# A graph network layer on one core: five buffers of rows of x, loaded ahead, and single rows fetched by SyncE for two more blocks

## The chip, the core and the metric

The kernel runs on one core of one Trainium2 chip. The time is device microseconds for one execution. A core has five engines, each with its own in-order queue of instructions: TensorE (PE in the profile; PEld are its weight loads) multiplies matrices, VectorE (DVE) and ScalarE (ACT) work elementwise, GpSimd (POOL) here only issues gathers, and SyncE (SP) here only issues transfers between memory and the on-chip buffers. An engine that waits for a semaphore holds up everything behind it in its own queue.

## The reference, cut to what matters

There are N = 8192 nodes with C = 256 features, and E = 131072 edges, sorted by their target, with 64 features each.

```
ea  = edge_attr @ w_e + b_e
msg = relu(x[src] + ea)                       # 131072 x 256: a gather of rows of x
agg = segment_sum(msg, dst, num_segments=N)
h_local = bn(relu((x + agg) @ w1 + b1) @ w2 + b2 + x)
h_attn  = bn(attention in groups of 32 nodes, 4 heads, of x, with in_w and out_w) + x, scaled likewise
out = h_local + h_attn
out = bn(out + relu(out @ m_w1 + m_b1) @ m_w2 + m_b2)
result = layernorm(x + out)
```

All of it is fp32. The batch norms (bn) are a scale and a shift for each feature.

## The kernel before, in words

**Edges.** The edges are worked on in 128 blocks of 1024 (BE). For a block, GpSimd issues eight indirect transfers, each of which gathers 128 rows of x into the tile xs (`gather`, line 217; the tile has six buffers). SyncE loads the block's edge features in four transfers (`load_edges`, line 261, tile ea, four buffers, up to four blocks ahead). VectorE transposes them in squares of 32 (line 299, tile eaT), TensorE multiplies them by w_e into PSUM (`edge_products`, tile pe), VectorE adds the gathered rows (`edge_messages`, line 357), ScalarE takes the relu (line 361). VectorE builds a one-hot matrix from the relative targets `rel` (`edge_hot`, line 369, tile oh), TensorE sums the messages with it (`group_sums`, tile pw), ScalarE copies the sums out (`edge_sums`, line 405, tile ws, two buffers), and TensorE places them by a second one-hot product (`edge_place`, tile l), which VectorE adds to the transposed x of the right nodes (line 431, tile xT).

**Single rows.** In the blocks of the list FETCHED (six in number, from 44 to 98) the eighth gather is left out. Its 128 rows are fetched by SyncE, one transfer of 1 KB for each row, from addresses that SyncE reads into registers: `row_stream`, line 239, tile xf with two buffers, in steps of four rows. A step is issued whenever the scheduler calls `between`, as long as there is a quota, and from about block 26 on each block adds three steps (RUN) to the quota. In these blocks the last addition is made in three pieces (line 351), two from xs and one from xf.

**Nodes.** The nodes are worked on in 16 chunks of 512 (CH). For a chunk, the rows of x are loaded by SyncE into the tile xn (`load_nodes`, line 438, four buffers). `attention_front` turns them by TensorE (line 178) into xT and computes q and k; `attention_back` computes v, the attention and its output product; `dense`, once all edges of the chunk are placed, computes the two layers of the local part and the two of the final one, adds the rows of xn at the end (line 748, the last reader of xn), normalises, and stores the result (line 765). The last two chunks are cut into smaller parts (`dense` of half chunks and `dense_rows`).

**Order.** TensorE's order is written out by the program while it is built. The class Work holds four streams of generators (dense parts, fronts, backs, and the second dense stream of the end); each `yield` gives the estimated time of what was just issued. Until block 24 (NV) VectorE's and ScalarE's order is written out too (`stated`). Up to block 104 (TAIL) blocks go in pairs, and `run` hands out a share of work between the steps of the edges. The last 24 blocks go singly: a planner with an assumed time at which each block's rows have come (`came`) decides what is next, and `step` hands out the node work between.

Some yields are signals. LOAD, from line 580, says that a front has just issued the load of its own rows: in the middle part the front's stream then rests until the program's own clock has gone on by 10 us (FAR), in the first part for two rounds, in the last part for 6 us. AFTER makes the back's stream wait for the next block, by the counter `told`, which counts only in the first part.

From chunk 4 on a front may begin only when `dense` of the chunk four before has been issued to its end. It then finds no rows of x loaded, issues the load (which on the chip waits until line 748 of that dense part has run, because the buffer is the same), and yields LOAD.

**Holding the gathers.** After the order is built, `hold_fetches` ties each gather to a matmul: the n-th gather waits for the last matmul whose estimated time lies 10 us (AHEAD) or more before n times 1.254 us.

Of the kernel before, what the change touches and what calls it, by code (L numbers as in the profile page):

```python
# [41 lines left out]
RUN = 3  # L42
FETCHED = [44, 54, 64, 76, 86, 98]
FROM = 26
# [44 lines left out]
def gnn_kernel(ctx: ExitStack, tc: tile.TileContext, x, src, dst, edge_attr, w, out):  # L89
# [27 lines left out]
    srci = const.tile([P, NB, TB], I32, name="srci")  # L117
    rel = const.tile([P, NB, TB], FP, name="rel")
    wrow = const.tile([P, NB], FP, name="wrow")
# [69 lines left out]
    def hold_fetches():  # L189
# [3 lines left out]
        for n, fetch in fetches:  # L193
# [8 lines left out]
            if i:  # L202
# [3 lines left out]
                )  # L206

    def gather(b):
        xs = epool.tile([P, NH, TJ, C], FP, name="xs", tag="xs", bufs=BUFS)
        for h in range(NH):  # L210
            for j in range(TJ):
                if b in FETCHED and h * TJ + j == TB - 1:
                    continue
                idx = srcd[:, b * NH + h, j : j + 1] if b < ND else srci[:, b, h * TJ + j : h * TJ + j + 1]
                fetches.append((
                    b * TB + h * TJ + j,
                    nc.gpsimd.indirect_dma_start(  # L217
                        out=xs[:, h, j, :],
                        out_offset=None,
                        in_=x if b < NX else xb[:, :],  # L220
                        in_offset=bass.IndirectOffsetOnAxis(ap=idx, axis=0),
                    ).ins,
                ))
        xs_of[b] = xs

    last_src = const.tile([P, P], I32, name="last_src")
    xf_of = {}

    def row_stream():

        for b in FETCHED:
            xf = xf_of[b] = epool.tile([P, C], FP, name="xf", tag="xf", bufs=2)
            for r in range(QR):
# [4 lines left out]
                for m, row in enumerate(rows):  # L238
                    nc.sync.dma_start(xf[m * QR + r : m * QR + r + 1, :], xb[ds(row, 1), :])  # L239
                yield  # L240

# [50 lines left out]
    def between():  # L292
        for do in spots:
            do()
# [39 lines left out]
    def edge_messages(b, pairs=range(0, NH, 2), of_pair=range(2)):  # L334
# [6 lines left out]
        for h in pairs:  # L341
            pe = pe_of[b, h]
            for u in of_pair[::n]:
                hs = slice(h + u, h + u + n)
                if h + u + n == NH and b in FETCHED:
                    for us, js, rows in (
                        (slice(0, 2), slice(0, TJ - 1), xs[:, h:]), (slice(0, 1), slice(TJ - 1, TJ), xs[:, h:]),
# [48 lines left out]
    def edge_sums(blocks):  # L396
# [3 lines left out]
        if pw is None:  # L400
            pw = pps.tile([P, 2, C], FP, name="pw", tag="at", bufs=4)
            for i, b in enumerate(blocks):
                group_sums(pw, i, b, [(h, j) for j in range(TJ) for h in range(NH)])
        ws = epool.tile([P, 2, C], FP, name="ws", tag="ws", bufs=2)
        newest["ws"] = nc.scalar.copy(ws[:, :n], pw[:, :n]).ins  # L405
# [27 lines left out]
    chunk = [{} for _ in range(NCH)]  # L433
    stated = [True]

    def load_nodes(n0, st, pool):
        xn = st["xn"] = pool.tile([P, TN, C], FP, name="xn", tag="xn", bufs=4)
        nc.sync.dma_start(xn, x[ds(n0, CH), :].rearrange("(t p) c -> p t c", p=P))
# [251 lines left out]
    def dense(n0, st, pool, bank, a=0, z=CH, own=("h1", "m1", "zT", "y", "")):  # L690

        assert st["done"]
        w, cs = z - a, slice(a, z)
        tiles = [(t // P, min(P, w - t)) for t in range(0, w, P)]
# [175 lines left out]
    class Work:  # L870
# [15 lines left out]
        def may(self, i):  # L886
            s = self.streams[i]
            return s and not self.rest[i] and self.told >= self.after[i] and clock[0] >= self.free[i] and s[0][0]()

# [29 lines left out]
        def step(self, t, until):  # L919

            n = len(self.streams)
            for i in [k % n for k in range(self.turn, self.turn + n)]:
                while self.streams[i] and self.streams[i][0][0]() and t >= self.at[i]:
# [4 lines left out]
                    elif d in (REST, LOAD):  # L928
                        self.at[i] = t + 6.0
                    elif d > 0:  # L930
                        t += d
                        self.at[i], self.turn = t + 0.5, (i + 1) % n
                        return t
            later = [a for a, q in zip(self.at, self.streams) if q and q[0][0]() and a > t]
# [13 lines left out]
    with tc.manual_schedule(engines={PE}):  # L948
# [136 lines left out]

        came = [8.7 + 10.035 * (i + 1) for i in range(NB)]
        t, l, s = came[b - 2] + 20, b - 2, b - 2
# [82 lines left out]
    hold_fetches()  # L1170
    fast.close()


# [121 lines left out]
```

## Time and profile before

| | |
|---|---|
| Median of 3 runs | 1645.59 us (1641.8 to 1648.5) |
| The profiled execution | 1641.08 us, span of its instructions 1639.3 us |
| Mean granted TensorE clock | 0.914 of full speed |
| DVE, ACT busy in the span | 805.6 us (49%), 591.8 us (36%) |
| Transfers | 240.62 MB, mean 147 GB/s |
| Gathers issued by GpSimd (line 217) | 858 + 144 + 16 = 1018 |
| Row transfers issued by SyncE (line 239) | 768 |
| Loads of chunks of x (line 438) | 16, the last at 1378.4 us |

The span runs from the first to the last instruction. A group of instructions is shown with its line, engine, operation, the names of its output and inputs, its count, its busy time, the mean of one in ns, and the idle time just before it with what ended that. A wait is shown as the engine and line that waited, what it waited for, the total, how often, and the longest. Times of instructions count from the span's start. The granted clock is TensorE's, as a share of full speed.

### The profile page before, as it was taken

What the parts mean: (1) busy time and instruction counts of PE and PEld (TensorE: products, weight loads), DVE (VectorE), ACT (ScalarE), POOL (GpSimd) and SP (SyncE); (2) the same over time, 40 slices, a digit from 0 to 9 for tenths busy, and PEclk for the clock granted to TensorE, in tenths of its full rate; (3) what the DMA queues carried; (4) which work ended last, traced back from release to release, by engine and by line L of the source; (5) the groups of instructions that cost most, each with busy time, mean ns of one, the idle gap of its engine ahead of it and who ended that gap; (6) DMA issues with size and microseconds to landing.
All of it is one profiled execution on the core that took longest, in us unless ns stands there. A gap on an engine that the chain in (4) does not pass through costs nothing. (4 is left out here: it accounts for less than half of the span.)

```text
span 1639.3 us, 24510 instructions
## 1 busy us (share of the span) xinstructions
PE 1330.6 (81%) x7591; PEld 762.6 (47%) x7591; DVE 805.6 (49%) x1649; ACT 591.8 (36%) x842; POOL 966.1 (59%) x1026
## 2 busy tenths in 40 slices
PE   3778769788987888778887588879799898878777
PEld 2444444444543545345553354445445454444555
DVE  5266664436454364345553355354455546364543
ACT  1334333333434344243442334324344343433333
POOL 5665656466666566656666465656666656656662
PEclk9888889899999999889998799889899899999899
DMA  9679755445545464454544545445565655454531
GB/s 240 181 220 262 222 148 148 131 130 152 152 126 164 112 163 129 127 150 132 150 127 126 136 130 147 123 130 145 132 164 138 160 124 163 128 142 123 148 97 50
DMA packets 150339, 240.62 MB, mean 147 GB/s; under 512 B 28638, under 2 KB 113788, under 8 KB 149436
## 3 DMA queue, kind: packets, MB, share of 16 engines
q0 software_dynamic: 48864, 133.50, 29.9%
q1 hardware_dynamic: 100252, 105.51, 23.3%
q8 instruction: 62, 1.02, 0.3%
q14 instruction: 73, 0.60, 0.1%
q10 hardware_dynamic: 1088, 0.00, 0.0%
HBM read 222.13 MB, written 16.78 MB: 146 GB/s over the span
## 5 line engine op out<-in xcount | busy, mean ns | idle before, releaser
L217 POOL DMA_INDIRECT xs<-xb,srci x858 | 811.9, 946 | 535.6 <-issue 211.3
L361 ACT ACTIVATE xs<-xs 128x1024 f32<-128x1024 f32 (+2 forms) x253 | 263.6, 1046 | 424.2 <-DVE xs L357 275.6
L357 DVE TENSOR_TENSOR xs<-pe,xs 128x1024 f32<-128x1024 f32 (+2 forms) x253 | 298.0, 1203 | 171.7 <-PE at L174 51.0
L174 PE MATMUL pe<-we,eaT 64*128 64x256 f32 x2048 | 314.0, 431 | 80.4 <-issue 39.3
L174 PEld LDWEIGHTS pe<-we,eaT 64*128 64x128 f32 x2048 | 211.7, 208 | 189.3 <-issue 105.6
L174 PE MATMUL pw<-xs,oh 128*32 128x256 f32 x2048 | 192.4, 416 | 53.0 <-issue 48.9
L217 POOL DMA_INDIRECT xs<-in_x_dram,srci x144 | 137.1, 952 | 95.5 <-issue 37.2
L369 DVE TENSOR_TENSOR oh<-iota_n,rel 128x128 f32<-128x128 f32 x256 | 65.4, 293 | 238.6 <-PE pw L174 94.6
L174 PEld LDWEIGHTS pw<-xs,oh 128*32 128x32 f32 x2048 | 71.3, 115 | 166.4 <-issue 132.7
L174 PE MATMUL at<-xT,inT 128*128 128x512 f32 x256 | 123.6, 609 | 5.4 <-issue 4.1
L174 PE MATMUL at<-hA,mw 128*128 128x512 f32 (+1 forms) x256 | 120.7, 599 | 3.3 <-DVE hA L714 1.4
L174 PE MATMUL at<-m,mw 128*128 128x512 f32 (+1 forms) x256 | 115.7, 594 | 8.8 <-ACT m L721 3.9
L174 PE MATMUL l<-oh,ws 128*128 128x160 f32 (+4 forms) x512 | 86.3, 309 | 30.3 <-ACT ws L405 15.0
L174 PEld LDWEIGHTS l<-oh,ws 128*128 128x128 f32 x512 | 75.3, 198 | 64.4 <-issue 35.0
L299 DVE STREAM_TRANSPOSE eaT<-ea 128x512 f32<-128x512 f32 x128 | 89.4, 699 | 30.3 <-PE at L174 9.8
L405 ACT COPY ws<-pw 128x512 f32<-128x512 f32 (+1 forms) x77 | 39.4, 511 | 151.7 <-remote 53.6
L640 ACT COPY pr<-pe 32x256 f32<-32x256 f32 x128 | 46.5, 363 | 91.8 <-remote 45.6
L174 PEld LDWEIGHTS at<-m,mw 128*128 128x128 f32 x256 | 48.4, 197 | 63.2 <-issue 53.9
L174 PE MATMUL at<-oT,outT 128*128 128x512 f32 x128 | 72.0, 691 | 6.5 <-ACT oT L675 3.8
L174 PEld LDWEIGHTS at<-xT,inT 128*128 128x128 f32 x256 | 47.6, 194 | 63.0 <-issue 55.7
L174 PE MATMUL at<-xT,w 128*128 128x512 f32 (+1 forms) x128 | 66.5, 655 | 11.4 <-DVE xT L431 8.6
L431 DVE TENSOR_TENSOR xT<-l,xT 128x352 f32<-128x352 f32 (+14 forms) x107 | 43.3, 427 | 59.4 <-remote 30.7
(163 smaller groups left out, 1270.2 us busy)
## 6 DMA issues: line engine op xcount, KB each, us to landing
ea<-in_edge_attr_dram SPq DMA_DIRECT2D x512, 128.0 KB
xs<-xb,srci POOLq DMA_INDIRECT x858
xf<-xb SPq DMA_DIRECT2D x768, 1.0 KB
xn<-in_x_dram SPq DMA_DIRECT2D x16, 512.0 KB
out_dram<-y SPq DMA_DIRECT2D x14, 512.0 KB
xp<-in_x_dram SPq DMA_DIRECT2D x10, 512.0 KB
xb<-xp SPq DMA_DIRECT2D x10, 512.0 KB
xp<-in_x_dram SPq DMA_DIRECT2D x3, 1024.0 KB
```

The source lines that it names most:

```text
L174: mark(ps, nc.tensor.matmul(ps, *args, **kw).ins)
L217: nc.gpsimd.indirect_dma_start(out=xs[:, h, j, :], out_offset=None, in_=x if b < NX else xb[:, :], in_offset=bass.IndirectOffsetOnAxis(ap= ...
L299: nc.vector.transpose(eaT, ea[:, QR:].rearrange("p (g d) -> p g d", d=ED)[:, :, :QR])
L357: nc.vector.tensor_add(msg[:, hs, js].rearrange("p u i c -> p i u c"), pe[:, js, u : u + n, :], xs[:, hs, js].rearrange("p u i c -> p i u c"),
L361: nc.scalar.activation(msg[:, hs, js], msg[:, hs, js], AF.Relu)
L369: nc.vector.tensor_tensor(oh[:, ts], iota_n[:, None, :WN].to_broadcast([P, TB // 2, WN]), rel[:, b, ts, None].to_broadcast([P, TB // 2, WN ...
L405: newest["ws"] = nc.scalar.copy(ws[:, :n], pw[:, :n]).ins
L431: newest["xT"] = nc.vector.tensor_add(xT, l2[:, :, a - n : z - n], xT).ins
L640: nc.scalar.copy(pr[q, :, 2 * hh : 2 * hh + 2, :].rearrange("p t s k -> p s t k"), two4[q, :, :, q])
```

## The change

- `xn` has five buffers instead of four. To make room, `ws` has one instead of two, and `rel` is bf16 instead of fp32 (its values are small whole numbers).
- `dense` of chunk c, when it begins, issues the load of the rows of chunk c + 4 (for chunks 4 to 15). The front of that chunk then finds its rows loaded and yields no LOAD. The first four chunks load as before.
- FETCHED also names blocks 108 and 117. So 1016 gathers and 1024 row transfers are issued. As these two blocks lie in the last 24, the planner's `step` now calls `between` too, so that rows are issued there, and a check is added that a block's rows have all been issued.
- `skipped(b)` counts the blocks of FETCHED from TAIL up to b. The planner's assumed arrival times (`came`) and the numbers by which later gathers are held are moved earlier by 1.254 us for each.
- A stream that waits for the next block (AFTER) is let go when the first part ends.

```
-FETCHED = [44, 54, 64, 76, 86, 98]
+FETCHED = [44, 54, 64, 76, 86, 98, 108, 117]
...
-    rel = const.tile([P, NB, TB], FP, name="rel")
+    rel = const.tile([P, NB, TB], BF, name="rel")
...
+    def skipped(b):
+        return sum(TAIL <= i <= b for i in FETCHED)
...
-                    b * TB + h * TJ + j,
+                    b * TB + h * TJ + j - skipped(b - 1),
...
+                if r == QR - 1:
+                    all_of.add(b)
...
+                    assert b in all_of
...
-        ws = epool.tile([P, 2, C], FP, name="ws", tag="ws", bufs=2)
+        ws = epool.tile([P, 2, C], FP, name="ws", tag="ws")
...
-        xn = st["xn"] = pool.tile([P, TN, C], FP, name="xn", tag="xn", bufs=4)
+        xn = st["xn"] = pool.tile([P, TN, C], FP, name="xn", tag="xn", bufs=5)
...
     def dense(n0, st, pool, bank, a=0, z=CH, own=("h1", "m1", "zT", "y", "")):
         assert st["done"]
+        if fast_path[0] and not a and n0 // CH + 4 < NCH:
+            load_nodes(n0 + 4 * CH, chunk[n0 // CH + 4], pool)
...
-            return s and not self.rest[i] and self.told >= self.after[i] and clock[0] >= self.free[i] and s[0][0]()
+            return s and not self.rest[i] and (self.told >= self.after[i] or not stated[0]) and clock[0] >= self.free[i] and s[0][0]()
...
                         self.at[i], self.turn = t + 0.5, (i + 1) % n
+                        between()
                         return t
...
-        came = [8.7 + 10.035 * (i + 1) for i in range(NB)]
+        came = [8.7 + 10.035 * (i + 1) - 1.254 * skipped(i) for i in range(NB)]
```

More of the change, by code (lines that the diff above doesn't have):

```diff
@@ L226, in gnn_kernel @@
     last_src = const.tile([P, P], I32, name="last_src")
-    xf_of = {}
+    xf_of, all_of = {}, set()
     def row_stream():
@@ L433, in gnn_kernel @@
     chunk = [{} for _ in range(NCH)]
-    stated = [True]
+    stated, fast_path = [True], [True]
     def load_nodes(n0, st, pool):
-        xn = st["xn"] = pool.tile([P, TN, C], FP, name="xn", tag="xn", bufs=4)
+        xn = st["xn"] = pool.tile([P, TN, C], FP, name="xn", tag="xn", bufs=5)
         nc.sync.dma_start(xn, x[ds(n0, CH), :].rearrange("(t p) c -> p t c", p=P))
@@ L1171, in gnn_kernel @@
     fast.close()
+    fast_path[0] = False
     wide = nc.values_load(width[0:1, 0:1])
```

## The prediction

> **What bounds the kernel now.** I read the page first, then who waited for whom on TensorE, then the instructions in order of time around the two longest waits, then the busy time by stretches. The page's head and the group of gathers:
>
> ```profile
> span 1639.3 us, 24510 instructions
> PE 1330.6 (81%) x7591; PEld 762.6 (47%) x7591; DVE 805.6 (49%) x1649; ACT 591.8 (36%) x842; POOL 966.1 (59%) x1026
> L217 POOL DMA_INDIRECT xs<-xb,srci x858 | 811.9, 946 | 535.6 <-issue 211.3
> ```
>
> TensorE is busy for 1330.6 of 1639.3 us and idle for 308.7. GpSimd is busy for only 59%, though the schedule in the code is written as if its gathers were the clock (10.035 us for each block of eight). How fast do the gathers really come? Two stretches of the gathers alone, the first from block 28 to the end of block 91, the second from block 96 to the end of block 123 (columns: length, POOL busy and count, clock, DMA share, GB/s):
>
> ```profile
> 373.50:1173.60 800.10, 479.70 (x507) 0.91 0.51 138
> 1220.90:1566.60 345.70, 211.02 (x223) 0.94 0.51 138
> ```
>
> The 507 gathers are 64 blocks of eight less five that SyncE replaced, 12.50 us a block; the 223 are 28 blocks less one, 12.35 us a block. So neither stretch runs at the gathers' pace. Each gather is held in the code until TensorE has reached a certain matmul, so the gathers follow TensorE, and I count what TensorE loses. Anything that leaves TensorE idle in its in-order queue in the middle of the kernel should reach the end almost in full.
>
> Most of its 308.7 idle us are small change: a few tenths between one operand's arrival and the next. Two single waits stand out, both by the transposes of a newly loaded chunk of x (tile xn, line 178); the waits of two windows:
>
> ```profile
> PE at L178 <- DMA xn<-in_x_dram: 5.3, 1, 5.3
> PE at L178 <- DMA xn<-in_x_dram: 16.2, 1, 16.2
> ```
>
> In order of time, first round the shorter wait and then round the longer one (start, duration, engine, line):
>
> ```profile
> 701.55 1.29 DVE L748 TENSOR_TENSOR y<-at,xn 128x512 f32<-128x512 f32 x2 [2.24 <-remote]
> 714.02 1.76 SPq L261 DMA_DIRECT2D ea<-in_edge_attr_dram  x4
> 718.97 0.28 SPq L438 DMA_DIRECT2D xn<-in_x_dram  x1
> 721.77 1.29 DVE L299 STREAM_TRANSPOSE eaT<-ea 128x512 f32<-128x512 f32 x2
> 724.03 1.97 PE L178 MATMUL at<-ident,xn 128*128 128x128 f32 x8 [5.26 <-DMA xn<-in_x_dram]
> ...
> 900.34 1.29 DVE L748 TENSOR_TENSOR y<-at,xn 128x512 f32<-128x512 f32 x2 [2.41 <-PE at L174]
> 907.87 2.14 SPq L261 DMA_DIRECT2D ea<-in_edge_attr_dram  x4
> 914.89 1.29 DVE L299 STREAM_TRANSPOSE eaT<-ea 128x512 f32<-128x512 f32 x2
> 915.61 1.80 SPq L261 DMA_DIRECT2D ea<-in_edge_attr_dram  x4
> 919.79 0.41 SPq L438 DMA_DIRECT2D xn<-in_x_dram  x1
> 924.38 1.97 PE L178 MATMUL at<-ident,xn 128*128 128x128 f32 x8 [16.20 <-DMA xn<-in_x_dram]
> ```
>
> The buffer of xn comes free when line 748 has added x to the last result of an old chunk: at 702.84 and at 901.63. The load is issued 16.1 and 18.2 us later, because SyncE issues in order and stands behind the loads of edge rows (line 261), which themselves wait for VectorE to transpose an older tile:
>
> ```profile
> SPq L261 <- DVE oh L369: 11.2, 1, 11.2
> ```
>
> Then the load needs 4.6 to 5.1 us to land, and TensorE, whose queue has the transposes next, stands. In the other ten of the twelve loads from chunk 4 on, the pause that the code puts behind a load (10 us of its own reckoning) covered it.
>
> **The change part by part.** *The early load.* With five buffers the load of chunk c+4 is issued at the beginning of the dense layers of chunk c. Its buffer is then that of chunk c-1, whose last reader is done or nearly so, and the transposes come behind the whole dense part of chunk c, tens of us later. The load is moved past the SyncE loads and the output store that stood ahead of it; nothing that was ahead of it needs it. So both waits go: 5.3 + 16.2 = **-21.5 us**.
>
> What comes after them goes too. Busy time and clock in the four us after each wait and the four after that (columns: length, then PE, PEld, DVE, ACT, POOL busy, granted clock, DMA share, GB/s), and the same eight transposes where nothing was late:
>
> ```profile
> 724.00:728.00 4.00, 3.97 (x11) 2.78 (x12) 0.00 (x0) 2.68 (x4) 0.00 (x0) 0.50 0.41 147
> 728.00:732.00 4.00, 4.00 (x10) 1.71 (x9) 0.00 (x0) 1.37 (x2) 1.90 (x2) 0.97 0.18 53
> 924.00:928.00 4.00, 3.62 (x24) 2.17 (x24) 0.00 (x0) 2.41 (x4) 0.00 (x0) 0.50 0.19 63
> 928.00:932.00 4.00, 4.00 (x37) 2.61 (x34) 2.51 (x4) 0.97 (x2) 2.35 (x3) 0.79 0.17 41
> 1208.14 1.04 PE L178 MATMUL at<-ident,xn 128*128 128x128 f32 x8
> ```
>
> After each wait TensorE worked at a granted clock of 0.50, and its eight transposes took 1.97 us for 1.04. What it lost is 4 x (0.50 + 0.03 + 0.50 + 0.21) = **-5.0 us**. The Trainium skill, page "TensorE: Matmul & The Clock Gate", section "Part 1: The HAM clock gate", says that an idle window of about 3.4 us halves the clock and that it takes about 3.4 us of work to get it back. By that figure the two waits would have cost 2 x 1.7 = 3.4 us instead of 5.0, and the sum below would be 1.6 us smaller; the 0.50 in the rows agrees with the rule.
>
> Against that stands what the kernel made good after a wait, since the gathers and VectorE had run ahead. The stretch from the transposes to the next line 748, after a load that wasn't late and after the two late ones:
>
> ```profile
> 522.80:585.00 62.20, 54.18 (x309) 30.42 (x306) 29.70 (x54) 24.76 (x36) 36.87 (x39) 0.92 0.48 128
> 724.00:782.00 58.00, 52.08 (x292) 31.18 (x294) 25.36 (x45) 22.53 (x32) 32.41 (x35) 0.90 0.48 132
> 924.40:986.00 61.60, 56.27 (x335) 33.12 (x336) 28.38 (x54) 25.98 (x37) 35.51 (x38) 0.90 0.48 128
> ```
>
> TensorE idles 12.9%, 10.2% and 8.7%. The difference, 2.7% of 58.0 and 4.2% of 61.6, is 4.2 us that were already won back: **+4.2 us**.
>
> *No pause behind the load.* The attention stream of the next chunk no longer stops for 10 us of reckoning behind its load, so its matmuls can fill that stretch. The first and the last of ten such stretches, from line 748 to the transposes, without the two above:
>
> ```profile
> 296.00:307.00 11.00, 4.43 (x9) 1.64 (x8) 6.15 (x20) 3.09 (x4) 5.06 (x6) 0.75 0.81 213
> 1377.00:1388.00 11.00, 8.28 (x46) 4.28 (x47) 9.21 (x25) 4.60 (x7) 6.49 (x7) 1.00 0.54 172
> ```
>
> All ten are 141.9 us long with 29.1 us idle; at 12.9% it would be 18.3. So 10.8 us is the most that filling them can give. The work that moves in is missing later in the same chunk, and the next dense part can't open before its edges are added up, so that some of the idleness only moves; a loss is bounded by the same size. I take **-3 us** of 0 to -10.8, nearer to none since about half of the excess (6.57 - 1.42 = 5.1 us) lies in the first stretch alone.
>
> *Two gathers fewer.* Blocks 108 and 117 lose one gather each, 946 ns of GpSimd: at most -1.9 us where GpSimd is the late one in the last stretch, nothing where TensorE is. I take **-1 us**. That the later gathers are let go 1.25 and 2.5 us earlier in the reckoning, and that the planner of the last 24 blocks expects them as much earlier, is the same gain seen from the other side and isn't counted again.
>
> In return the last addition of those two blocks is made in three pieces. The whole one, and the pieces as they ran in the six blocks that have them now (the second number behind the bar is the mean in ns):
>
> ```profile
> L357 DVE TENSOR_TENSOR xs<-pe,xs 128x1024 f32<-128x1024 f32 x248 | 295.3, 1216 | 171.3 <-PE at L174 51.0 <-issue 27.2 <-PE pw L174 26.2
> L351 DVE TENSOR_TENSOR xs<-pe,xs 128x512 f32<-128x512 f32 x6 | 4.1, 681 | 1.0 <-PE pw L174 1.0
> L351 DVE TENSOR_TENSOR xs<-pe,xf 128x256 f32<-128x256 f32 x6 | 2.5, 413 | 0.0
> L351 DVE TENSOR_TENSOR xs<-pe,xs 128x256 f32<-128x256 f32 x6 | 2.5, 413 | 0.0
> L369 DVE TENSOR_TENSOR oh<-iota_n,rel 128x128 f32<-128x128 f32 x256 | 65.4, 293 | 238.6 <-PE pw L174 94.6 <-remote 68.4 <-PE pe L174 45.6
> ```
>
> 681 + 413 + 413 - 1216 = 291 ns, twice: **+0.6 us**, if VectorE is waited for both times.
>
> *256 more single rows.* They are SyncE transfers of one row each, 64 steps of four, three steps to a block, so they occupy SyncE in some 21 more blocks: today's stream ends at 1195.6 us and would now end some 21 x 12.35 = 260 us later, near 1460. What such rows take in SyncE's queue, at their usual and at their slowest, and the edge loads that stand behind them:
>
> ```profile
> L239 SPq DMA_DIRECT2D xf<-xb x768: 2/228/1387, 253.1 to 1195.6; - x192
> ...
> xf<-xb SPq DMA_DIRECT2D x768, 1.0 KB
> 637.82 7.90 SPq L239 DMA_DIRECT2D xf<-xb  x12
> 878.60 14.41 SPq L239 DMA_DIRECT2D xf<-xb  x12
> 893.11 1.76 SPq L261 DMA_DIRECT2D ea<-in_edge_attr_dram  x4
> ```
>
> Behind a late row stand the next edge rows and the output stores; who waits for those is VectorE's transposition (line 299) and then TensorE. The cover is that edge rows are loaded up to four blocks ahead. I take 0: the stretch with rows at 12.50 us a block contains the 21.5 us of the two waits, and without them it is (800.1 - 21.5) / 64 = 12.17, not slower than the 12.35 of the stretch that has almost no rows. If the cover fails, see the last rival.
>
> *The rest at nothing.* The one-hot comparison (line 369) reads a bf16 operand instead of fp32 and still writes fp32; it took 293 ns, and a tenth either way would be 256 x 29 ns = 7.5 us on VectorE, which is 49% busy, so a us or two at the end. With one buffer instead of two for ws, ScalarE's copy must wait for the matmuls that read the former ws; these stand ahead of the sums that the copy reads anyway in TensorE's in-order queue, so the wait is over before it begins. The relaxed rule for a stream that waits for the next block, once the written-out order ends, adds no instruction.
>
> The sum: -21.5 - 5.0 + 4.2 - 3.0 - 1.0 + 0.6 = **-25.7 us**. The profiled execution took 1641.08 us with its span of 1639.3, so it would take 1615.4. The median of the runs shown is 1645.59, 4.5 above it, so I forecast **1620 us** for the runs.
>
> **The rivals.** *More is filled.* If all ten stretches fill up (-10.8), nothing had been made good (0 for +4.2) and both gathers count, the sum is -21.5 - 5.0 - 10.8 - 1.9 + 0.6 = -38.6: 1607 us. For it speaks that the order gets smoother in every chunk; against it, that a dense part still waits for its edges.
>
> *Another wait stands behind the one removed.* VectorE's transposes of edge rows (line 299) ended at 721.77 + 1.29 = 723.1 us and at 914.89 + 1.29 = 916.2, that is 4.3 and 8.0 us into the two waits (which began at 724.03 - 5.26 = 718.8 and at 908.2). If the edge products come next in TensorE's order and these transposes are as late as before, only 21.5 - 12.3 = 9.2 us go. Half the clock loss stays (-2.5), half the catch-up (+2.1), and the sum with the small terms at none is -9.6 + 0.6 = -9.0: 1637 us, at the edge of no difference. For it: VectorE sat idle in the longer wait itself. Against it: the chunk's own sixteen attention matmuls come first and give TensorE some 10 us of work.
>
> ```profile
> L174 PE MATMUL at<-xT,inT 128*128 128x512 f32 x256 | 123.6, 609 | 5.4 <-issue 4.1 <-ACT xT L588 1.3
> ```
>
> (256 over 16 chunks, times 609 ns, is 9.7 us.)
>
> *Slower: the rows crowd SyncE in the last third.* If twelve rows take 14.41 us as at their slowest, a block needs 14.41 + 1.76 = 16.2 us of SyncE, against 12.35 that it lasts. Over 21 blocks SyncE would fall behind by 81 us, the edge rows would come late and all engines with them: 1620 + 81 = 1701 us. It decides from 12.35 - 1.76 = 10.6 us for twelve rows on; 7.90 is below, 14.41 above, and the mean of the two is 11.2. To eat the gain and half a per cent more, twelve rows must take 12.2 us on average. Against it speaks the pace of 12.17 us a block with rows. The Trainium skill, page "DMA: Bandwidth & Descriptors", section "Rules for kernel authors", speaks against this part of the change: many small transfers should be one large one, since below 64 KB a transfer is mostly overhead. The trace agrees as to the overhead (7.90 us for 12 KB) and not that it reaches the end.
>
> **How the numbers follow.** About half a per cent, 8 us, is what a measurement of this kernel can tell from no change. The forecast case, 0.53, and the fuller one, 0.18, are faster. The second rival, 0.17, lies on the edge: 0.05 of it faster, 0.12 the same. The crowded queue has 0.12 and is slower. So faster 0.76, same 0.12, slower 0.12. The range goes from 1607 less the spread of the runs (3.8 below their median), some 1602, to the second rival plus it and its unknown small terms, 1642; the slower case is left out, and a little on either side.
>
> **What would show it.** Right: no wait of line 178 for xn, issues of line 438 some 60 to 100 us ahead of the transposes, no stretch at clock 0.50 in the middle, TensorE's idle time down by about 24 us with its busy time a few us shorter, and a block pace near 12.2 us before and after 1196 us. The single rows go on to about 1460 us. Wrong: a new wait of TensorE of over 5 us in the same places, this time for eaT; edge loads that land after VectorE wants them while the rows of blocks 108 and 117 are fetched; or gaps that open ahead of the dense parts, as large as those that close behind the loads.

## The result, and the profile after

The change makes the kernel slower: 1700.82 us, the median of four runs (1697.94 to 1705.88), against 1643.69 us for the kernel before on the same chip (four runs, 1637.57 to 1648.5). The ratio is 1.0353, with a 95% interval of 1.0309 to 1.0397. The profiled execution took 1697.94 us. I had forecast 1620.

The page's head of the changed kernel, its groups of edge products and of additions to xT, and its transfers of single rows:

```profile
span 1695.8 us, 25335 instructions
PE 1319.3 (78%) x7591; PEld 770.1 (45%) x7591; DVE 810.0 (48%) x1653; ACT 591.8 (35%) x842; POOL 964.2 (57%) x1024
L174 PE MATMUL pe<-we,eaT 64*128 64x256 f32 x2048 | 331.8, 456 | 219.2 <-DVE eaT L305 134.0
xf<-xb SPq DMA_DIRECT2D x1024, 1.0 KB
```

TensorE is busy for 11 us less than before, but idle for 376.5 us instead of 308.7. Did the two waits for xn go? The view of the tile xn in the changed kernel, what its readers waited for:

```profile
its engine sat idle before it (us, times) until:
  PE at L178: 7.8, 7
  PE pe L174: 4.2, 1
  issue: 1.9, 3
  PE at L800: 1.7, 1
```

No transfer is named any more: the rows of x are always there. But the group of edge products above now waits 134.0 us for eaT, VectorE's transposed edge rows. The same wait in the view of waits, first of the kernel before, then of the changed one:

```profile
PE pe L174 <- DVE eaT L299: 3.0, 1, 3.0
```

```profile
PE pe L174 <- DVE eaT L305: 134.0, 32, 10.7
```

One wait of 3 us has become 32 waits with a sum of 134. Does VectorE in turn wait for the edge rows to land? The view of line 305 in the changed kernel, what ended VectorE's idle time ahead of the 128 transposes:

```profile
its engine sat idle before it (us, times) until:
  remote: 9.0, 2
  issue: 3.3, 1
  DMA ea<-in_edge_attr_dram: 1.2, 1
  PE l L174: 0.8, 1
```

It does so once, for 1.2 us. So the edge rows are in time, and VectorE is busy with something else when TensorE wants them turned. One of the longest waits in order of time, in the changed kernel:

```profile
1038.93 1.11 PE L174 MATMUL pw<-xs,oh 128*32 128x256 f32 x16
1039.43 1.76 SPq L267 DMA_DIRECT2D ea<-in_edge_attr_dram  x4
1039.45 0.29 DVE L376 TENSOR_TENSOR oh<-iota_n,rel 128x128 f32<-128x128 f32 x1 [6.70 <-PE pe L174]
1039.66 0.68 DVE L653 TENSOR_REDUCE mx<-pr 128x16 f32<-128x512 f32 x1
1040.45 0.89 DVE L656 TENSOR_TENSOR pr<-pr,mx 128x128 f32<-128x128 f32 x4
1041.26 2.35 DVE L364 TENSOR_TENSOR xs<-pe,xs 128x1024 f32<-128x1024 f32 x2
1041.93 7.67 SPq L243 DMA_DIRECT2D xf<-xb  x12
1043.53 0.67 DVE L660 TENSOR_REDUCE sm<-pr 128x16 f32<-128x512 f32 x1
1045.33 0.95 DVE L663 TENSOR_TENSOR pr<-pr,sm 128x128 f32<-128x128 f32 x4
1046.32 2.85 DVE L667 STREAM_TRANSPOSE bd<-pr 32x512 f32<-32x512 f32 x4
1046.80 0.94 POOL L221 DMA_INDIRECT xs<-xb,srci  x1 [0.30 <-issue]
1049.20 0.71 DVE L305 STREAM_TRANSPOSE eaT<-ea 128x512 f32<-128x512 f32 x1
1050.06 3.79 PE L174 MATMUL pe<-we,eaT 64*128 64x256 f32 x16 [10.01 <-DVE eaT L305]
1052.41 0.94 POOL L221 DMA_INDIRECT xs<-xb,srci  x1 [4.66 <-PE pe L174]
```

At 1040.04 the edge products of the next block are next in TensorE's in-order queue. Their eaT stands in VectorE's queue behind the additions of the block before (line 364) and behind the whole softmax of the chunk's attention (lines 653 to 667). Ten us later it comes, and GpSimd, whose gather is tied to these products, has lost 4.66 us. VectorE wasn't short of time: it stood idle for 6.70 us ahead of the one-hot of line 376 (the row at 1039.45), while this eaT, whose edge rows SyncE had issued at 1002 to 1004 us, was further back in the same queue.

The wait costs more than its ten us. In the four us behind it the granted clock is 0.50, and the 16 edge products take 3.79 us, where undisturbed ones of the kernel before take 2.00 (at 1081.21). Seven waits behind a softmax between 734 and 1369 us (8.4 to 10.7 us each) all have 0.50 to 0.52 behind them: the clock loss that the prediction took off has come back too.

In the kernel before, in the softmax of the same chunk, the transpose stands ahead of the last step (bd, there line 660):

```profile
1068.71 0.65 DVE L299 STREAM_TRANSPOSE eaT<-ea 128x512 f32<-128x512 f32 x1
1070.17 2.85 DVE L660 STREAM_TRANSPOSE bd<-pr 32x512 f32<-32x512 f32 x4
```

So nothing that the change moves on purpose is late, and VectorE's queue has another order. That order isn't written in the code after block 24: it is made when the program is built, by a scheduler that goes by its own estimates. In the two built programs, and in the traces' order of time as well, the transpose of block k stands ahead of the additions of block k-1 nearly throughout before (after the written-out part, all but blocks 53 to 55 and 69 to 70, the blocks at the two waits for xn). In the changed program it stands behind the first of them, and mostly behind all, from block 51 to 118.

Where the time goes, by the first gather of a block (us; counted through the gathers in order of time, eight to a block, seven in fetched ones), on this chip:

| kernel | blocks 64 to 80 | 80 to 104 | 104 to 120 |
|---|---|---|---|
| before | 206.6 | 295.5 | 202.2 |
| after | 209.8 | 317.9 | 222.7 |

The first stretch holds the 16.2 us wait of the kernel before, and still it is 3.2 us longer without that wait: the gain is eaten on the spot. In the next two no wait for xn was to be gained, and 22.4 and 20.5 us are lost. Another 6.7 us are lost between blocks 50 and 64, where the shorter wait stood (180.7 us for 174.0).

### The profile page after: what moved, and what is told of

Its sections match the earlier page's. It is cut to its first block, busy times and chain, and to the rows that moved or that the text cites. A ratio compares the mean times of both kernels' runs of the same rounds, so it can differ in the third digit from the quotient of the medians.

```text
span 1695.8 us, 25335 instructions
## 1 busy us (share of the span) xinstructions
PE 1319.3 (78%) x7591; PEld 770.1 (45%) x7591; DVE 810.0 (48%) x1653; ACT 591.8 (35%) x842; POOL 964.2 (57%) x1024
## 3 DMA queue, kind: packets, MB, share of 16 engines
q8 instruction: 62, 1.02, 0.3%
## 5 line engine op out<-in xcount | busy, mean ns | idle before, releaser
L174 PE MATMUL pe<-we,eaT 64*128 64x256 f32 x2048 | 331.8, 456 | 219.2 <-DVE eaT L305 134.0
L368 ACT ACTIVATE xs<-xs 128x1024 f32<-128x1024 f32 (+1 forms) x251 | 262.0, 1046 | 521.6 <-DVE xs L364 278.9
L364 DVE TENSOR_TENSOR xs<-pe,xs 128x1024 f32<-128x1024 f32 (+1 forms) x251 | 296.2, 1204 | 200.6 <-PE pe L174 70.9
L174 PEld LDWEIGHTS pe<-we,eaT 64*128 64x128 f32 x2048 | 230.3, 221 | 329.7 <-issue 232.3
L174 PE MATMUL pw<-xs,oh 128*32 128x256 f32 x2048 | 183.5, 415 | 40.9 <-issue 38.2
L174 PEld LDWEIGHTS pw<-xs,oh 128*32 128x32 f32 x2048 | 67.8, 115 | 142.0 <-issue 108.9
L174 PE MATMUL at<-m,mw 128*128 128x512 f32 (+1 forms) x256 | 119.3, 607 | 3.4 <-ACT m L730 2.6
L174 PEld LDWEIGHTS at<-hA,mw 128*128 128x128 f32 x256 | 48.5, 203 | 62.4 <-issue 52.2
L174 PE MATMUL at<-oT,outT 128*128 128x512 f32 x128 | 66.9, 638 | 5.5 <-issue 4.9
```

What stands on the lines that cost most here:

```text
L174: mark(ps, nc.tensor.matmul(ps, *args, **kw).ins)
L364: nc.vector.tensor_add(msg[:, hs, js].rearrange("p u i c -> p i u c"), pe[:, js, u : u + n, :], xs[:, hs, js].rearrange("p u i c -> p i u c"),
L368: nc.scalar.activation(msg[:, hs, js], msg[:, hs, js], AF.Relu)
```

## The experiments

My theory now: single rows and early loads together change the built order of VectorE's queue, eaT falls behind longer work, and TensorE and the gathers wait for it. The rivals: the rows crowd SyncE (the slower case of the prediction), the early load by itself does harm, or the pause that fell away was needed.

Eight of the kernels ran on two chips on which the kernel before takes 1327 and 1330 us (the fast chips below), six on two on which it takes 1627 and 1639, near the 1644 of the first (the first kind); so each is compared with the kernel before on its own chip, and stretches of blocks only within one kind of chip.

**One part at a time.** First the early load with the six old blocks of rows:

```
-FETCHED = [44, 54, 64, 76, 86, 98, 108, 117]
+FETCHED = [44, 54, 64, 76, 86, 98]
```

> The change with the six old blocks in FETCHED: five buffers and the early load, no rows for blocks 108 and 117. Order theory (in the built program VectorE's transposition of a block's edge rows, eaT, stands behind all additions of the block before it instead of ahead of the second-last ones, from block 51 on, and TensorE waits for it): here it stands so for blocks 51 to 99, not to 119, some 50 of 68 blocks. The change lost 1701 - 1620 = 81 us against the forecast, 1.2 us for each of 68 blocks; so 1620 + 50 x 1.2 = 1680 us, about 90 to 100 us of TensorE waiting for eaT, none of it after block 102. SyncE theory (the added rows crowd SyncE in the last third on the chip): no added rows, so about 1620. Pause theory (the missing pause behind the load crowds the fronts): the pause is missing in every chunk, so about 1700 as with the whole change.

Measured: 1360.31 against 1326.85 us, a ratio of 1.0245 (1.0217 to 1.0274), with 71.6 us of waits for eaT. Blocks 64 to 104 take 425.0 us, against 396.4 in rows_eight, the next kernel, on the same chip; behind the rows, from 104 to 120, it takes 164 us, near the 160 of 128 gathers at 1.25 us.

Then all of the change but the early load:

```
-        if fast_path[0] and not a and n0 // CH + 4 < NCH:
-            load_nodes(n0 + 4 * CH, chunk[n0 // CH + 4], pool)
```

> The change without the early load: rows of blocks 108 and 117 by SyncE, five buffers of which one isn't needed, the load and its pause as before. Order theory: VectorE's queue has eaT where it was before, so 1643 within 10 us, TensorE waiting for eaT under 10 us, and the two waits for xn back. SyncE theory: all 256 rows are there, so about 1700. Pause theory: 1643.

Measured: 1327.62, a ratio of 0.9999 (0.9987 to 1.0012). The view of its waits:

```profile
PE at L178 <- DMA xn<-in_x_dram: 20.4, 2, 13.6
PE pe L174 <- DVE eaT L305: 3.6, 2, 2.3
```

The 256 further rows, the bf16 `rel`, the single buffer of ws, the two gathers fewer and the planner's new times together cost nothing on this chip. The two waits for xn are back, and those for eaT are gone. Rows alone, then, don't crowd SyncE enough to cost time.

The whole change and the early load without any rows, side by side:

> The whole change once more, beside the others. Where the kernel before takes 1327 us, its gathers run at 1.25 us each without a gap, so that nothing can be won there by filling TensorE; the six-block version lost 33 us by eaT standing late for 50 blocks, 0.67 us a block. Order theory: 68 blocks x 0.67 = 45 us, ratio 1.034 (where the kernel before takes 1640 us: 1.035 as first measured). SyncE theory (rows crowd it on the chip): more than that, the rows of the last third being new. Pause theory: as the six-block version, 1.025, plus little.

> Early load and five buffers, but no block in FETCHED: all 1024 gathers by GpSimd, no single rows at all. eaT stands 5.3 us of work ahead of the former block's last addition. Order theory: no waits for eaT; where the gathers are the bound, six more of them at 1.25 us, so 1327 + 8 = 1335 us, ratio 1.006. Pause theory: the pause is missing, so 1.025 plus 0.006 = 1.031.

```
-FETCHED = [44, 54, 64, 76, 86, 98, 108, 117]
+FETCHED = []
```

Measured: the change 1395.57 against 1330.48 us, 1.048 (1.0447 to 1.0513), with 104.7 us of waits for eaT. The early load without rows 1339.06, 1.0069 (1.0044 to 1.0094), with 2.3 us of them; it has six gathers more than the kernel before, which at 1.25 us each are 7.5 of its 8.6 us. So on these chips the early load alone does no harm, and the pause, which is gone here too, wasn't needed. Rows alone cost nothing, early loads alone nothing, both together 4.8%. In the built programs, and in the traces, eaT keeps its place in the two harmless ones and falls behind in the other. TensorE's order isn't the cause: the traces of early_six and early_without_rows show the same 7591 matmuls in the same order, and only the first of the two is slow.

The change itself was a miss: the order theory had 1.034 for it, and more than that was said to speak for a crowded SyncE. The added loss lies mostly in blocks 104 to 120, which take 194.4 us here, 164.0 in early_six and 157.9 in rows_eight. rows_eight fetches the same rows, and in change_again eaT waits for edge rows once, 1.4 us; so the crowding isn't seen here either. What else stands in those blocks comes below.

**Misses.** Three kernels were to show directly that the place of eaT carries the loss. One tied the additions of a block behind the transpose issued last:

> The whole change, with one ordering edge more: from block 24 on the additions of a block stand behind the transposition eaT that the program issued last, in VectorE's queue. Nothing else is changed. Order theory: TensorE's waits for eaT fall from 134 us to under 15, and the time comes to what was forecast, 1610 to 1630. SyncE theory and pause theory: the rows and the missing pause are still there, so 1690 to 1710.

```
+        turned_at[0] = nc.vector.transpose(eaT, ...).ins
...
+        with tc.issue_after(turned_at[0]):
+            messages(b, pairs, of_pair)
```

Measured: 1.1112 (1.108 to 1.1145). The tie held the other way round: eaT stayed late and drew the additions with it, and TensorE waited 150.0 us for xs instead. It told nothing of the change.

Two others made eaT late in the kernel before, first directly behind the additions and then about as far behind them as in early_six:

> The kernel before, with one thing changed: for blocks 51 to 104 eaT is issued one step later in the program and tied behind the last addition of the block before it, as in the changed kernel. No early load, no added rows, the pause kept. Order theory: slower by about 54 blocks x 1.2 us = 65 us, some 1700 us, with 100 us or more of TensorE waiting for eaT. SyncE theory and pause theory: nothing that they name is there, so 1643.

```
+            if 50 <= b < 106:
+                behind.enter_context(tc.issue_after(added_at[0]))
             nc.vector.transpose(eaT, ...)
...
-                next_edges(b + 2)
+                if b < 50:
+                    next_edges(b + 2)
+                elif b > 50:
+                    next_edges(b + 1)
...
```

> The kernel before, with eaT of blocks 51 to 104 issued later in the program and tied behind whatever VectorE was given last: the addition of the former block, the one-hot, the last dense and the last softmax instruction. It then stands 2.5 us of VectorE's work behind the former block's last addition, as in the six-block version of the change (2.5); directly behind it (1.2) it cost nothing. Early load, rows and pause are as before the change. Order theory: 1.02 to 1.03, with 60 us or more of waits for eaT. Pause theory and SyncE theory: 1.00.

```
+                for ins in (added_at[0], hot_at[0], newest["xT"], newest["dense"], soft_at[0]):
+                    behind.enter_context(tc.issue_after(ins))
...
```

Measured: 1.000 (0.9986 to 1.0014) with 31.6 us of waits for eaT, and 1.003 (1.0018 to 1.0042) with 59.8 us; I had expected some 65 us more of the first and 1.02 to 1.03 of the second. So neither the late place by itself nor the sum of TensorE's waits for eaT is the price. What differs is whether the waits reach the gathers. GpSimd's waits for the edge products, in later_in_before and in the change on the same chip:

```profile
POOL xs L217 <- PE pe L174: 28.2, 59, 10.5
```

```profile
POOL xs L221 <- PE pe L174: 85.2, 71, 9.7
```

On these chips the gathers set the pace (126 gathers in 158.0 us, 1.25 us each, in blocks 64 to 80 of rows_eight), and a wait of TensorE that wasn't passed on to a held gather was made good. The sizes fit: GpSimd waits 26.4 us for the edge products in rows_eight, which loses nothing, 28.0 more in early_six, which loses 33.5, and 58.8 more in the change, which loses 65.1. My theory was too coarse: not that eaT is late, but which wait holds a gather.

One more issues the edge rows from ScalarE's queue, to unload SyncE:

> The whole change, but from block 40 on the loads of edge rows are issued from ScalarE's queue instead of SyncE's. Rows, early load and missing pause are all kept. In the built program VectorE's transposition eaT then stands 5 us of VectorE's work ahead of the former block's last addition (kernel before: 4.6 ahead; changed kernel: 3.3 behind it). Order theory: TensorE's waits for eaT fall under 15 us and the ratio to the kernel before is 1.00 or, where TensorE is the bound, 0.98 to 0.99; if ScalarE is held up by the waits of the loads, up to 1.01. Pause theory: the pause is still missing, so 1.025 or more.

```
-                nc.sync.dma_start(
+                (nc.scalar if b >= 40 else nc.sync).dma_start(
```

Measured: 1.040 (1.0366 to 1.0434), where I had expected 1.01 at most. The waits for eaT fell to 2.3 us, but ScalarE, which now issues the loads, waited for them (54.4 us ahead of m and 41.3 ahead of ws), and TensorE waited 52.5 us for bd. One wait in exchange for another: it decides nothing between the theories.

**Which early loads.** In the built program the order falls behind in other blocks if only some chunks are loaded early, or if the rows come at another pace. That makes a forecast of the place. The three kernels are early_to_7, early_from_11 and, with every early load but fewer rows, early_run2:

```
-        if fast_path[0] and not a and n0 // CH + 4 < NCH:
+        if fast_path[0] and not a and n0 // CH + 4 < NCH and n0 // CH + 4 < 8:
```

```
-        if fast_path[0] and not a and n0 // CH + 4 < NCH:
+        if fast_path[0] and not a and n0 // CH + 4 < NCH and n0 // CH + 4 > 10:
```

```
-RUN = 3
-FETCHED = [44, 54, 64, 76, 86, 98, 108, 117]
+RUN = 2
+FETCHED = [44, 64, 86, 108, 117]
```

> The change with the early load for chunks 4 to 7 alone; the other eight chunks are loaded in the first part of their own work, as before, and all eight blocks of single rows are kept. In the built order VectorE's transposes eaT keep their place ahead of the additions from block 55 on. Order theory: one wait for eaT behind the softmax near block 50, none after it; ratio 1.000 to 1.006. Rival (each early load beside single rows costs the same, 65 us over twelve): four of them, 22 us, a ratio of 1.016.

> The change with the early load for chunks 11 to 15 alone. In the built order eaT keeps its place up to block 81 and falls behind the additions and the softmax from block 82 to 118. Order theory: blocks 64 to 80 at the pace of the kernel without early loads (79.6 us for eight), blocks 88 to 104 at 85 us for eight, and the slow stretch from 104 to 120 (194 us instead of 160) as in the whole change: 45 to 55 us, a ratio of 1.034 to 1.042. Rival (each early load costs the same): five of twelve, 27 us, 1.02.

> The change with SyncE's single rows spread thinner: two steps of four rows for each block instead of three, for five blocks (44, 64, 86, 108, 117) instead of eight. In the built order eaT falls behind from block 74 to 112. Three more gathers than the kernel before with its six blocks cost one, 1.25 us. Order theory: no wait for eaT before block 74, from there 5.7 us lost in each eight blocks up to 112, 27 us, a ratio of 1.02 to 1.03. Rival (the crowding of SyncE by rows is the price): two thirds of the rows at a time leave it uncrowded, 1.000 to 1.006.

Measured: early_to_7 1.0058 (1.0029 to 1.0088), early_from_11 1.0374 (1.0317 to 1.043), early_run2 1.0128 (1.0088 to 1.0168), all against 1639.23 us. (The sizes that I had expected were reckoned with block times of the fast chips, where the change costs 4.8%; these ran on the first kind, where it costs 3.5%. What the runs test is the place.) Five early loads with a late order cost as much as twelve, four with the order kept from block 55 on cost a sixth of it. The waits for eaT come where the built order said. In early_to_7 the edge products wait for eaT once, for 10.0 us, ahead of 700 us, and not again. In early_from_11 there is none up to 1019 us, where block 80 begins, and from there to 1500 us:

```profile
PE pe L174 <- DVE eaT L305: 77.6, 19, 9.2
```

In early_run2 none up to 930 us (the first gather of block 72 is at 911); from 930 to 1100 and from 1100 to 1500 us:

```profile
PE pe L174 <- DVE eaT L305: 13.6, 6, 6.2
...
PE pe L174 <- DVE eaT L305: 43.8, 13, 10.1
```

Its whole is smaller than I expected (20 us for 27): from block 64 to 80 it takes 195.8 us, eleven less than the kernel before with its wait for xn, which I had left out of the reckoning. It lies between the two theories in size, and with the first in place.

**One thing moved.** In the change the same pattern comes back every eight blocks, one chunk: one wait behind the softmax (7.5 to 7.7 us on the fast chip, 8.4 to 10.7 on the first), and some three shorter ones, most of them of about 1.5 us. So I queued only the second half of the softmax behind the transpose that it had overtaken:

```
+        with ExitStack() as behind:
+            if not stated[0] and fast_path[0]:
+                behind.enter_context(tc.issue_after(turned_at[-2]))
             sm = pool.tile([P, TN * H], FP, name="sm", tag="sm")
...
             nc.vector.transpose(bd[q, :, :, g, :]...)
```

> The whole change, with one thing moved on VectorE: the second half of the softmax (the sum, the reciprocal, the products and the transposes bd, some 4.9 us) is queued behind the transpose eaT of the block whose products come next, instead of ahead of it. Nothing is left out. Once in every chunk of eight blocks the change makes TensorE wait 7.5 to 7.7 us for eaT behind that half of the softmax, and the next gather is let go 4.7 us late; eight blocks then take 85.3 us instead of 79.6 between blocks 64 and 104. Theory (this one place is the price): the wait shrinks to under 3 us, eight blocks take 80 to 81.5 us, and the whole kernel 25 to 45 us less than the change: a ratio to the kernel before of 1.015 to 1.03 instead of 1.048. Rival (the price is spread over the whole rearranged queue, or lies in the early loads themselves): the wait moves to the next instruction, eight blocks stay above 84 us and the ratio at 1.04 or more.

Measured: 1674.13 against 1639.23 us, 1.0216 (1.0169 to 1.0262). This too ran on the kind of chip where the change costs 3.5%, so that the rival stands at about 1.035 and not at the 1.04 or more that was expected of it; the measured ratio lies below that all the same. The same place in its order of time:

```profile
1029.56 2.34 DVE L365 TENSOR_TENSOR xs<-pe,xs 128x1024 f32<-128x1024 f32 x2
1033.52 0.70 DVE L306 STREAM_TRANSPOSE eaT<-ea 128x512 f32<-128x512 f32 x1
1034.15 0.65 DVE L664 TENSOR_REDUCE sm<-pr 128x16 f32<-128x512 f32 x1
1034.37 3.79 PE L174 MATMUL pe<-we,eaT 64*128 64x256 f32 x16 [4.89 <-DVE eaT L306]
1036.07 2.85 DVE L671 STREAM_TRANSPOSE bd<-pr 32x512 f32<-32x512 f32 x4
1037.13 0.94 POOL L221 DMA_INDIRECT xs<-xb,srci  x1 [1.08 <-PE pe L174]
```

TensorE waits 4.89 us instead of 10.01, and the held gather loses 1.08 instead of 4.66. Blocks 80 to 104 take 302.6 us instead of 317.9, though the transposes are still behind the additions. But blocks 104 to 120 stay at 223.1. There another long piece stands ahead of eaT, the normalisation of y (the longest wait in that stretch of softmax_behind):

```profile
1497.52 1.38 DVE L773 TENSOR_SCALAR y<-y,mv,rstd 128x256 f32<-128x256 f32 x4
1498.81 0.70 DVE L306 STREAM_TRANSPOSE eaT<-ea 128x512 f32<-128x512 f32 x1
1499.57 3.75 PE L174 MATMUL pe<-we,eaT 64*128 64x256 f32 x16 [7.86 <-DVE eaT L306]
```

So I moved that too, once with all eight blocks of rows and once with the six old ones:

```
+            if not stated[0] and fast_path[0]:
+                behind.enter_context(tc.issue_after(turned_at[-1]))
             for wt, ts in groups:
                 nc.vector.reciprocal(rstd[:wt, ts], rstd[:wt, ts])
             for t, wt in tiles:
                 nc.vector.tensor_scalar(y[:wt, t, :], ...)
```

> The change with two things moved on VectorE: the second half of the softmax behind the transpose eaT of the block next in line, as in softmax_behind, and the end of the dense layers (line 767's reciprocal and line 769's four normalisations of y, 1.6 us and a wait for ScalarE) behind the newest eaT. Nothing is left out. With the softmax alone moved, blocks 64 to 104 took 505 us against 528 in the change and 502 in the kernel before, but blocks 104 to 120 stayed at 223 us against 222 and 202; there the two longest waits for eaT (6.5 and 7.9 us) stood behind y. Theory (single long pieces ahead of eaT are the price, in the last stretch those of y): blocks 104 to 120 come to 205 to 214 us, the whole to a ratio of 1.005 to 1.015. Rival (in the last stretch something else binds, such as the single rows or the pieces with fetched rows): 104 to 120 stay over 219 us, and the ratio at 1.02.

> The same two moves, with single rows for the six old blocks alone: the early load, mended as far as it can be, without the late rows. In the built order eaT is late only from block 52 to 100. Theory: blocks 64 to 104 at the pace of the kernel before or a few us under it, since the two waits for xn are gone, and blocks 104 to 120 at its 202 us: a ratio of 0.99 to 1.003. Rival (the early load costs even with eaT ahead of the softmax and of y): 1.01 or more.

Measured: both_behind 1641.58 against 1627.14 us, 1.011 (1.0071 to 1.015); six_behind 1624.98, 0.9993 (0.9972 to 1.0014). All on chips of the first kind, by stretches (us, of one profiled execution each; the kernel before takes 1643.69 us where the first two ran, 1639.23 at the next four and 1627.14 at the last two, so up to 1% of a stretch, about two us in 200, can be the chip's):

| kernel | blocks 64 to 80 | 80 to 104 | 104 to 120 | ratio |
|---|---|---|---|---|
| before | 206.6 | 295.5 | 202.2 | 1 |
| after | 209.8 | 317.9 | 222.7 | 1.0353 |
| early_to_7 | 194.6 | 301.2 | 204.0 | 1.0058 |
| early_from_11 | 209.1 | 311.5 | 232.3 | 1.0374 |
| early_run2 | 195.8 | 309.7 | 211.2 | 1.0128 |
| softmax_behind | 201.9 | 302.6 | 223.1 | 1.0216 |
| both_behind | 196.7 | 294.7 | 209.8 | 1.011 |
| six_behind | 198.3 | 294.5 | 197.1 | 0.9993 |

With two pieces of VectorE's work put back behind eaT, two thirds of the loss is gone (3.53% before, 1.1% left). TensorE runs its 7591 matmuls in the same order in both traces, and the early loads and the rows are the same; so VectorE's order carries these two thirds. Without the late rows nothing is lost any more; what that kernel would lose without the two moves was measured on a fast chip alone (early_six, 2.45%). What is left of eaT's waits in both_behind and in six_behind:

```profile
PE pe L174 <- DVE eaT L306: 85.3, 29, 7.0
```

```profile
PE pe L174 <- DVE eaT L306: 54.0, 18, 6.7
```

These may be why six_behind isn't faster than the kernel before, though both waits for xn are gone, and why both_behind still loses 1.1%; no run takes them out, so that isn't shown. No version here beats the kernel before.

## Why the prediction was wrong

*What bounds the kernel.* That the two waits stood in TensorE's queue was right, and that SyncE's order made the load late. The why was half read: the row of 11.2 us that I showed is from the shorter wait. Round the longer one SyncE waited only 1.6 us for eaT, and single rows stood ahead of the load as well (eleven from 896.09 to 906.42 us, then four, then four more). What I didn't ask is what else these waits did.

*-21.5, -5.0 and +4.2 for the waits.* The waits went as I said, and in blocks 64 to 80, where the longer one stood, the two kernels with least of either kind of wait take 194.6 us (early_to_7, with 4.5 us left for xn) and 195.8 (early_run2, with 3.9 for eaT), against 206.6 before: 11 to 12 us of the 16.2 that I had counted there. **The step that failed** is that I priced the moved load by SyncE's queue alone: it "is moved past the SyncE loads and the output store that stood ahead of it; nothing that was ahead of it needs it". With it went the silent assumption that every other queue keeps its order, a term put at nothing without a reason. VectorE's order is made anew for each program, and I never compared it. There 134.0 us of waits for eaT took the place of 21.5, the half clock came back behind the long ones, and the kernel lost 57 us where I had forecast a gain of 25.7. Putting back two pieces of that order alone took the loss from 3.53% to 1.1%.

*-3 for the pause.* early_without_rows has no pause either and takes what its gathers cost more. But it ran where the gathers set the pace, so that work filled in on TensorE could gain nothing there. The term is neither shown nor refuted; a loss by the missing pause isn't seen.

*-1 and +0.6 for the gathers and the pieces, the rest at nothing.* rows_eight has all of these: 0.9999 (0.9987 to 1.0012), on a fast chip. Their sum of -0.4 us lies within that interval; the single terms can't be told apart.

*0 for the 256 rows.* Right for SyncE and wrong for the kernel. rows_eight shows that as transfers they cost nothing on a fast chip, and in the changed kernel twelve of them took 7.67 us (the order of time above), not the 14.41 of my slower case. But with the early load they keep the late order up to block 118 instead of 100: both_behind against six_behind, the same but for the two blocks, is 1.011 against 0.9993, and 12.7 us of it lie in blocks 104 to 120.

*The rivals.* The slower case gave 1701 us and the runs 1700.82, but by a mechanism that the runs refute: its edge rows came late, and on the chip they came in time. The number is a coincidence. The case "another wait stands behind the one removed" named the right wait. It priced it at 12.3 us in two places, because I took eaT to be as late as before and TensorE's chain at two points to be all that matters. Among the signs of being wrong, "a new wait of TensorE of over 5 us in the same places, this time for eaT" is what the profile shows, except for the places: it comes back in every chunk.

*What stays open.* Why the scheduler puts eaT later once the waits for xn are gone is argued, not shown. The order falls behind only while rows are fetched and only where loads are early, and in the kernel before it does so only at the two waits; this fits an estimate in which SyncE is full with rows and edge loads, and in which TensorE's waits for xn had given it time to catch up. The chip, in which eaT waits for no edge rows after the start, doesn't share that estimate. Nor is it known why the order falls behind only from block 51 on, though rows are fetched from about block 26. What makes up the 1.1% that both_behind still loses is open. Nor was it tried what the late order in the kernel before costs on a chip of the first kind, where later_in_before might have cost more than 0.3%.

## What to carry to other kernels

When the order of an engine's queue is made by a scheduler at build time, a wait that is taken out can reorder queues that the change doesn't touch: compare the built orders of all engines before you price the edit. Where something else sets the pace, a wait of an engine costs as far as it is passed on to that: 59.8 us of waits for eaT cost 0.3% in later_in_before, 104.7 us cost 4.8% in the change. So look at whose release a wait delays (here 4.66 us of a held gather) and not at the sum of the waits. And where many small waits appear at once, find the one long piece of work that has slipped ahead of a short one that others wait for; to move that piece alone is a cheap test of the cause.

## What the hardware did that I hadn't expected

The same program, the kernel before, took 1627 to 1646 us at the first measurement and on two chips later, and 1327 to 1330 us on two others. The profiled executions on the slower kind have a lower granted clock (0.914 in the kernel before, 0.959 in rows_eight on a fast chip). TensorE there has gaps between matmuls for which no releaser is seen ("issue"), and the matmuls themselves are a little longer. The group of the sums of messages, of the kernel before on the first chip and of rows_eight on a fast one (the same 2048 matmuls):

```profile
L174 PE MATMUL pw<-xs,oh 128*32 128x256 f32 x2048 | 192.4, 416 | 53.0 <-issue 48.9 <-DMA xs<-xb,srci 1.4 <-ACT xs L361 0.9
```

```profile
L174 PE MATMUL pw<-xs,oh 128*32 128x256 f32 x2048 | 137.7, 388 | 1.6 <-ACT xs L368 1.6
```

What makes the difference between the chips no run here tells. The change is slower on both kinds, by 3.5% and by 4.8%.
